# Layer 1's attention scores as pairs of 64-row tiles in fixed, adjacent PSUM banks

## The chip, the cores and the metric

The kernel runs on one core of one Trainium2 chip. The metric is device time in microseconds (us) of the whole program, the median of the runs shown. The engines go by short names: PE is TensorE's matrix multiply and PEld its weight load, DVE is VectorE, ACT is ScalarE, POOL is GpSimd; SP is the queue that issues all the DMAs here. PSUM is the memory that PE writes its results to and that DVE and ACT read them from.

## What is computed

Two transformer layers, each with an attention part and a feed-forward part, between modulated layer norms, over 2 sequences of 512 tokens with 512 channels. Layer 0's attention is a chunked linear attention (32 query heads of width 128 in 8 groups, chunks of 128 tokens) with a gate. Layer 1's is a plain softmax attention with 32 query heads of width 16, four of which share one of 8 key heads. Its feed-forward part mixes four streams with a 4x4 matrix that 50 Sinkhorn iterations make doubly stochastic. The change touches layer 1's attention:

```python
x = x + ga * attention0(h)                   # layer 0
x = x + gb * ffn0(layernorm(x) * (1 + cb) + sb)

xq = (x @ wq + bq).reshape(B, S, 32, 16)     # layer 1
xk = (x @ wk + bk).reshape(B, S, 8, 16)
xv = (x @ wv + bv).reshape(B, S, 8, 16)
q, k = _rope(xq, cos, sin), _rope(xk, cos, sin)
k, v = jnp.repeat(k, 4, axis=2), jnp.repeat(xv, 4, axis=2)
scores = jnp.einsum('bqhd,bkhd->bhqk', q, k) / jnp.sqrt(16.0)
probs = jax.nn.softmax(scores, axis=-1)
out = jnp.einsum('bhqk,bkhd->bqhd', probs, v)
...
H_res = sinkhorn_log(H_res_logits)           # 50 iterations, per token 4x4
```

## The kernel before

**Layer 0** runs as 64 units (L1305 and after): a unit is one group of four heads, one sequence and one chunk of 128 tokens. Every float product is made exact by three passes of rounded halves (`passes`, L227 to 234; the matmuls are all on L233). A unit asks for a gate tile (`gate`, PSUM name `gps`), for projections of queries, keys and values (`project`, `pps`), for scores (`sps`), a state (`cps`), a mixed output (`yps`), its transpose (`ztp`) and an output projection (`ops`). Each of these is one bank-sized PSUM tile of 128x512 floats, each name may have two at once, and all names share one pool: a scheduler, which plans the order of every engine's queue ahead of time from a model of the machine, gives a tile room when its first writer comes up and frees it after its last reader. `bank` (L155) is the helper through which `gps`, `pps`, `ops` and a few others are asked for. Weights come through staging tiles named `raw` (`raw_tile`, L199), of which there are `RAW` = 4: a DMA fills one, ACT rounds it to the high half (L210), POOL subtracts to get the low half (L211), and it is free again. `mod_load` (L266) takes up to four of them at once for the modulation rows.

**Layer 1's attention** runs as 128 pieces: two sequences, two halves of 256 queries, four pairs of key heads (`t`), and within each of these 16 steps eight pieces. Three pieces are put behind each of the last 11 units of layer 0, up to 33 (`FIRST`, `PER`, `HOLD`, L1343); the rest follow layer 0. A piece has two parts, and `weigh` runs ten pieces behind `maxima`.

`maxima` (L834) finds each query's largest score, which the softmax subtracts. The queries of two key heads lie in one tile of 96 partitions, 48 for each key head (high, high and low parts of 16 numbers), and each key head has a key tile of its own, zero in the other head's rows. So one matmul over 96 rows gives the scores of one key head, 128 queries by 512 keys, in a PSUM tile `s1` (three at once), and one DVE instruction (L847) reduces it:

```python
for qt in range(NQ):
    ps = psp.tile([P, L], FP, name="s1", bufs=S1)
    anchor["pe"] = nc.tensor.matmul(
        ps, lhsT=st["qs"][rp][0:KS, i, qt * P:(qt + 1) * P], rhs=st["ks"][s][0:KS], ...
```

A piece holds two such matmuls (two query tiles) and two reductions. After every fourth piece the maxima are split in two halves (L853, L854), transposed into `mt` (L857), copied by ACT to `mm` (L862) and written by one DMA (L863) into rows 96 to 99 of the query tile, where rows of ones in the key tile subtract them.

`weigh` (L865) makes the scores again, transposed, 128 keys by 256 queries at a time, over 100 rows (L877): per piece two PSUM tiles `s2` (three at once), each of two matmuls, and for each one ACT exponential (the `pt` rows on L68, the line of the helper that records ACT's instructions). `outputs` (L887, L897) multiplies four pieces' weights by the values, in four column tiles of 32 columns, into `op`; `finish` (L911) transposes that into `ot`, divides and adds it to the residual. `aside` (L1190) lets the Sinkhorn work of finished tokens run two steps per piece.

Of the kernel before, what the change touches and what calls it, by code (L numbers as in the profile page):

```python
# [21 lines left out]
RAW = 4  # L22
# [3 lines left out]
UPO = 600  # L26
SPLIT0, SPLIT1 = 16, 16
# [26 lines left out]
def tile_adaln(ctx: ExitStack, tc: tile.TileContext, a: dict, out: bass.AP):  # L54
# [62 lines left out]

    anchor = {}
# [35 lines left out]

    def bank(shape, name, bufs=2):  # L155
        return psp.tile(shape, FP, name=name, bufs=bufs)
# [576 lines left out]

    Q = L // 2
    NQ = Q // P
    KS, KM = 96, 100
# [4 lines left out]
    def layer1_keys(js=(0, 1)):  # L741
        for s in range(2):
            empty = temp([P, L], FR, "hi1")
            nc.scalar.copy(empty, raw_tile(a["c_keys1"][s]))
            for j in js:
                ksd[j, s] = temp([P, L], FR, f"ks{j}{s}")
                nc.sync.dma_start(out=ksd[j, s].bitcast(FP), in_=empty.bitcast(FP))
# [39 lines left out]
    def key_rows(i):  # L787
        j = key_tile(i)
        if j == 2 and (2, 0) not in ksd:
            layer1_keys((2,))  # L790
        return [ksd[j, s] for s in range(2)]

    def keys1(i):
        b, t = order[i]["b"], order[i]["t"]
        order[i]["ks"] = key_rows(i)
        holder[key_tile(i)] = i
        for s in range(2):
            nc.sync.dma_start(out=order[i]["ks"][s].bitcast(FP)[48 * s:48 * s + 48], in_=k_dram[b][2 * t + s])

    def queries1(i):  # L800

        b, half, t = (order[i][n] for n in ("b", "half", "t"))
        assert l1c["there", b]
        pair = []
        for rp in range(2):
            qs = temp([P, 2, Q], FR, "qs", QS)
            for s in range(2):
                h = 8 * t + 4 * s + 2 * rp
                nc.sync.dma_start(
                    out=qs.bitcast(FP)[48 * s:48 * s + 48],  # L810
                    in_=q_dram[b][h:h + 2, :, half * Q:half * Q + Q].rearrange("r k q -> k r q"),
                )
            pair.append(qs)
        return pair
# [18 lines left out]

    def maxima(st, k):  # L834

        assert holder[key_tile(st["i"])] == st["i"]
        rp, j = divmod(k, 4)
        s, i = divmod(j, 2)
        if j == 0:
            st["m"] = small.tile([P, NQ * 2, 2], FP, name="m")  # L840
        for qt in range(NQ):
            ps = psp.tile([P, L], FP, name="s1", bufs=S1)
            anchor["pe"] = nc.tensor.matmul(  # L843
                ps, lhsT=st["qs"][rp][0:KS, i, qt * P:(qt + 1) * P], rhs=st["ks"][s][0:KS],
                start=True, stop=True,
            ).ins
            anchor["dve"] = nc.vector.tensor_reduce(  # L847
                st["m"][:, 2 * qt + s, i:i + 1], ps, AX.X, ALU.max, negate=True
            ).ins
        if j == 3:  # L850
# [12 lines left out]
            anchor["sp"] = nc.sync.dma_start(out=st["qs"][rp].bitcast(FP)[96:100], in_=mm.bitcast(FP)).ins  # L863

    def weigh(st, k):  # L865

        assert holder[key_tile(st["i"])] == st["i"]
        rp, r = divmod(k, 4)
        kp, s = divmod(r, 2)
        if r == 0:  # L870
            quads.append({"st": st, "rp": rp, "pt": {}})
        qd = quads[-1]
        for i in range(2):
            ps = psp.tile([P, 2, Q], FP, name="s2", bufs=S2)
            for j in range(2):
                kt = 2 * kp + j
                nc.tensor.matmul(  # L877
                    ps[:, j, :], lhsT=st["ks"][s][0:KM, kt * P:(kt + 1) * P], rhs=st["qs"][rp][0:KM, i, :],
                    start=True, stop=True,
                )  # L880
# [6 lines left out]
    def outputs(j):  # L887
# [6 lines left out]
        with tc.high_priority(UPO):  # L894
            for kt in range(NC):
                for r in (3, 0, 1, 2):
                    mm = nc.tensor.matmul(  # L897
                        op[32 * r:32 * r + 32, :], lhsT=va[st["b"]][kt // 2][:, kt % 2, 2 * st["t"] + r // 2, :],
                        rhs=qd["pt"][r, kt // 2][:, kt % 2, :], start=kt == 0, stop=kt == NC - 1,
# [306 lines left out]
    at = [0]  # L1206
# [224 lines left out]
```

## Time and profile before

| | |
|---|---|
| three runs | 1408.99, 1407.75, 1398.83 us; median 1407.75 |
| the profiled execution | 1409.56 us, of which the trace's span is 1407.8 |
| mean granted TensorE clock | 0.944 of full |
| busy, share of the span | PE 89%, PEld 70%, DVE 83%, ACT 59%, POOL 56% |
| first and last maxima matmul (L843) | 898.4, 1261.4 us |
| first and last weighing matmul (L877) | 925.1, 1275.6 us |
| last matmul of layer 0 (`ops`) | 1033.8 us |

The same profile in 40 slices of 35.2 us, each digit the busy share in tenths:

```profile
PE   6979999999999999999988998899998899994117
DVE  7998668687677687787999977788699879888998
ACT  5456576476476466666665655567567467653226
PEclk9999999999999999999999999999999899986568
```

PE is at its top through layer 0 and through most of layer 1's attention. After 1276 us only the last tokens' Sinkhorn iterations and the last mixing are left, a stretch of 132 us in which DVE does most. A busy PE isn't the same as a PE that takes a new matmul as early as it can: a matmul's duration includes the time in which it runs through the array, and consecutive ones overlap. What a matmul costs the next one is the distance from start to start, which the timeline shows.

### The profile page before, as it was taken

To read this page: it belongs to the slowest core of one execution; us is meant where nothing else is said; L and a number is where in the kernel's file an instruction comes from. 1 tells how busy PE (TensorE), PEld (TensorE's weight loads), DVE (VectorE), ACT (ScalarE), POOL (GpSimd) and SP (SyncE) were. 2 spreads that over 40 slices of the span, in tenths; PEclk is the share of its full clock that TensorE was granted. 3 is DMA by queue.
4 is the path that set the end of the run, shared out by engine and by line. 5 is a ranking of instruction groups with operands and counts; after the bars stand their busy time and mean duration, and the time that the engine had idled before them with its cause. 6 is when DMAs were issued, how large, how long until landed. Compare 5 with 4: busy or idle time off the path is not lost. (4 is left out here: it accounts for less than half of the span.)

```text
span 1407.8 us, 23038 instructions
## 1 busy us (share of the span) xinstructions
PE 1247.3 (89%) x7128; PEld 990.5 (70%) x7128; DVE 1164.4 (83%) x3171; ACT 825.1 (59%) x2333; POOL 787.2 (56%) x1180
## 2 busy tenths in 40 slices
PE   6979999999999999999988998899998899994117
PEld 3767888788788778888876777677776667762116
DVE  7998668687677687787999977788699879888998
ACT  5456576476476466666665655567567467653226
POOL 4363274365264367577777757644243644657854
PEclk9999999999999999999999999999999899986568
DMA  7121241231131233224333327623212331100001
GB/s 241 36 70 43 87 124 39 68 106 53 53 118 56 94 117 111 81 79 128 120 106 90 98 70 233 179 66 97 65 42 94 101 92 48 59 2 1 1 15 46
DMA packets 95378, 117.14 MB, mean 83 GB/s; under 512 B 10828, under 2 KB 50508, under 8 KB 95256
## 3 DMA queue, kind: packets, MB, share of 16 engines
q1 hardware_dynamic: 95256, 115.67, 27.6%
q8 instruction: 57, 0.93, 0.3%
q14 instruction: 65, 0.53, 0.1%
HBM read 102.11 MB, written 10.64 MB: 80 GB/s over the span
## 5 line engine op out<-in xcount | busy, mean ns | idle before, releaser
L847 DVE TENSOR_REDUCE m<-s 128x1 f32<-128x512 f32 x256 | 166.6, 673 | 21.8 <-PE s L843 21.5
L68 ACT ACTIVATE pt<-s 128x512 f32<-128x512 f32 x256 | 137.4, 601 | 33.1 <-PE s L877 31.5
L448 POOL TENSOR_TENSOR q<-xcos,rot 128x512 f32<-128x512 f32 x64 | 92.8, 1450 | 56.5 <-DVE xcos L446 52.5
L68 ACT ACTIVATE sg<-sg 128x512 f32<-128x512 f32 x128 | 80.7, 632 | 64.5 <-DVE sg L479 62.5
L496 POOL TENSOR_SCALAR_AFFINE_SELECT dec<-gb 128x512 f32<-128x512 f32 x64 | 48.3, 755 | 121.2 <-DMA gb<-g_dram 65.4
L843 PE MATMUL s<-ks,qs 96*128 96x512 f32 x256 | 104.9, 442 | 11.5 <-DVE m L847 7.6
L877 PE MATMUL s<-qs,ks 100*128 100x256 f32 x512 | 104.4, 309 | 10.2 <-DMA qs<-mm 6.8
L233 PE MATMUL pps<-hh,wq_h 128*128 128x512 f32 x256 | 103.3, 403 | 7.1 <-ACT vT L767 3.4
L877 PEld LDWEIGHTS s<-qs,ks 100*128 100x128 f32 x512 | 82.7, 199 | 32.8 <-issue 7.9
L68 ACT ACTIVATE dec<-dec,room 128x128 f32<-128x128 f32 x256 | 83.0, 398 | 34.8 <-POOL dec L496 34.6
L233 PE MATMUL ops<-wo_h,zh 128*128 128x512 f32 x256 | 102.2, 399 | 1.2 <-ACT zh L571 1.0
L233 PE MATMUL gps<-wg_h,hh 128*128 128x512 f32 x256 | 101.3, 398 | 1.5 <-ACT wg_h L210 1.2
L233 PE MATMUL ops<-wo_h,zl 128*128 128x512 f32 x256 | 101.5, 396 | 0.7 <-DVE zl L572 0.7
L233 PE MATMUL pps<-hl,wq_h 128*128 128x512 f32 x256 | 101.8, 398 | 0.0
L233 PE MATMUL pps<-hh,wq_l 128*128 128x512 f32 x256 | 101.5, 397 | 0.0
L233 PE MATMUL gps<-wg_l,hh 128*128 128x512 f32 x256 | 101.1, 395 | 0.0
L233 PE MATMUL ops<-wo_l,zh 128*128 128x512 f32 x256 | 100.6, 393 | 0.0
L233 PE MATMUL gps<-wg_h,hl 128*128 128x512 f32 x256 | 100.6, 393 | 0.0
L516 POOL TENSOR_TENSOR gb<-gb,q 128x512 f32<-128x512 f32 x48 | 62.3, 1299 | 60.3 <-ACT gb L68 46.7
L549 PE MATMUL yps<-v,dec 128*128 128x128 f32 x512 | 93.4, 278 | 2.7 <-DVE xcos L446 1.4
L555 ACT ACTIVATE z<-yps 128x128 f32<-128x128 f32 x256 | 67.5, 278 | 41.1 <-PE yps L551 30.5
L559 DVE SCALAR_TENSOR_TENSOR z<-yps,ss,sg 128x128 f32<-128x128 f32 x256 | 72.0, 340 | 22.5 <-ACT ss L68 22.3
(321 smaller groups left out, 3984.4 us busy)
## 6 DMA issues: line engine op xcount, KB each, us to landing
gb<-g_dram SPq DMA_DIRECT2D x64, 256.0 KB
raw<-in_wq SPq DMA_DIRECT2D x56, 256.0 KB
raw<-in_wg SPq DMA_DIRECT2D x48, 256.0 KB
raw<-in_wo SPq DMA_DIRECT2D x48, 256.0 KB
raw<-in_wmod SPq DMA_DIRECT2D x40, 256.0 KB
qs<-q_dram SPq DMA_DIRECT2D x64, 96.0 KB
q_dram<-hi SPq DMA_DIRECT2D x16, 256.0 KB
raw<-in_wk SPq DMA_DIRECT2D x14, 256.0 KB
```

The costliest lines, as they stand in the source:

```text
L68: ins = nc.scalar.activation(o, i, func, **kw)
L233: nc.tensor.matmul(ps, lhsT=l, rhs=r, start=i == 0, stop=i == n - 1)
L448: nc.gpsimd.tensor_tensor(dst, sp(xc_), sp(rot), ALU.add)
L496: anchor["pool"] = nc.gpsimd.affine_select(out=dec, in_=gb, pattern=[[0, REP0], [1, P]], compare_op=ALU.is_ge, fill=-1e30, base=0, channel ...
L516: nc.gpsimd.tensor_tensor(gb, gb, q[:, c], ALU.mult)
L549: nc.tensor.matmul(yps[:, h, :], lhsT=u["pr"][:, h, :], rhs=u["v"][:, c, :], start=True, stop=not c)
L555: nc.scalar.activation(z[:, h, :], yps[:, h, :], AF.Square, accum_out=ss[:, h:h + 1])
L559: nc.vector.scalar_tensor_tensor(z[:, h, :], yps[:, h, :], ss[:, h:h + 1], sg[:, h * P:(h + 1) * P], ALU.mult, ALU.mult)
L843: anchor["pe"] = nc.tensor.matmul(ps, lhsT=st["qs"][rp][0:KS, i, qt * P:(qt + 1) * P], rhs=st["ks"][s][0:KS], start=True, stop=True,).ins
L847: anchor["dve"] = nc.vector.tensor_reduce(st["m"][:, 2 * qt + s, i:i + 1], ps, AX.X, ALU.max, negate=True).ins
L877: nc.tensor.matmul(ps[:, j, :], lhsT=st["ks"][s][0:KM, kt * P:(kt + 1) * P], rhs=st["qs"][rp][0:KM, i, :], start=True, stop=True,)
```

## The change

The two key heads of a step move to two halves of one tile: head 0 in partitions 0 to 47, head 1 in 64 to 111, with the rows of the maxima and of ones in 48, 49 and 112, 113. A matmul now works on 48 (or 50) rows that start at partition 0 or 64, and the two heads' matmuls follow each other directly, each into a bank of its own. The key tiles become half as many.

In `maxima` a piece is one pair of matmuls, one for each key head, of the same query tile, and one reduction over both banks gives both maxima. In `weigh` a piece is one pair, each 128 keys by 512 columns (two query heads at once) in place of four matmuls of 256 columns. The maxima go out by two DMAs, one for each half.

The reduction needs the two banks to lie side by side, so two pairs of banks, `pair0` and `pair1`, are set aside for the whole program. Until the first piece, the gate's tiles (`gps`) take turns in the two banks of `pair0`; until piece 48 (`ROOM2`), the projections' (`pps`) take turns in `pair1`. Pieces 0 to 47 use `pair0` alone, the later ones both in turn. The staging tiles `raw` go from four to three.

```diff
-RAW = 4
+RAW = 3
+ROOM2 = 48
...
+    pairs2 = [psp.tile([P, 2, L], FP, name=f"pair{k}", bufs=1) for k in range(2)]
+    turn2 = [0, 0]
     def bank(shape, name, bufs=2):
+        k = {"gps": 0, "pps": 1}.get(name)
+        if k is not None and (n_done[0] == 0 if k == 0 else n_done[0] < ROOM2):
+            turn2[k] += 1
+            return pairs2[k][:, turn2[k] % 2]
         return psp.tile(shape, FP, name=name, bufs=bufs)
...
-    KS, KM = 96, 100
+    KS, KM = 48, 50
...
-            nc.sync.dma_start(out=order[i]["ks"][s].bitcast(FP)[48 * s:48 * s + 48], in_=k_dram[b][2 * t + s])
+            nc.sync.dma_start(out=order[i]["ks"].bitcast(FP)[64 * s:64 * s + KS], in_=k_dram[b][2 * t + s])
...
+    def score_room(n):
+        return pairs2[n % 2 if n >= ROOM2 else 0]
     def maxima(st, k):
...
-        s, i = divmod(j, 2)
+        i, qt = divmod(j, 2)
...
-        for qt in range(NQ):
-            ps = psp.tile([P, L], FP, name="s1", bufs=S1)
+        pss = score_room(8 * st["i"] + k)
+        for s in range(2):
             anchor["pe"] = nc.tensor.matmul(
-                ps, lhsT=st["qs"][rp][0:KS, i, qt * P:(qt + 1) * P], rhs=st["ks"][s][0:KS],
-                start=True, stop=True,
+                pss[:, s], lhsT=st["qs"][rp][64 * s:64 * s + KS, i, qt * P:(qt + 1) * P],
+                rhs=st["ks"][64 * s:64 * s + KS], start=True, stop=True,
             ).ins
-            anchor["dve"] = nc.vector.tensor_reduce(
-                st["m"][:, 2 * qt + s, i:i + 1], ps, AX.X, ALU.max, negate=True
-            ).ins
+        anchor["dve"] = nc.vector.tensor_reduce(
+            st["m"][:, 2 * qt:2 * qt + 2, i], pss, AX.X, ALU.max, negate=True
+        ).ins
...
-            anchor["sp"] = nc.sync.dma_start(out=st["qs"][rp].bitcast(FP)[96:100], in_=mm.bitcast(FP)).ins
+            for s in range(2):
+                anchor["sp"] = nc.sync.dma_start(
+                    out=st["qs"][rp].bitcast(FP)[64 * s + KS:64 * s + KM], in_=mm.bitcast(FP)[4 * s:4 * s + 4]
+                ).ins
     def weigh(st, k):
...
-        for i in range(2):
-            ps = psp.tile([P, 2, Q], FP, name="s2", bufs=S2)
-            for j in range(2):
-                kt = 2 * kp + j
-                nc.tensor.matmul(
-                    ps[:, j, :], lhsT=st["ks"][s][0:KM, kt * P:(kt + 1) * P], rhs=st["qs"][rp][0:KM, i, :],
-                    start=True, stop=True,
-                )
+        pss = [psp.tile([P, 2, Q], FP, name="s2", bufs=S2) for s in range(2)]
+        for s in range(2):
+            nc.tensor.matmul(
+                pss[s], lhsT=st["ks"][64 * s:64 * s + KM, kt * P:(kt + 1) * P], rhs=st["qs"][rp][64 * s:64 * s + KM],
+                start=True, stop=True,
+            )
+        for s in range(2):
             p = wts.tile([P, 2, Q], FP, name="pt", bufs=PT)
-            anchor["act"] = qd["last"] = act(p, ps, AF.Exp, scale=0.25)
-            qd["pt"][2 * s + i, kp] = p
+            anchor["act"] = qd["last"] = act(p, pss[s], AF.Exp, scale=0.25)
+            qd["pt"][s, kt] = p
...
-    at = [0]
+    at = n_done
```

More of the change, by code (lines that the diff above doesn't have):

```diff
@@ L116, in rsqrt @@
         nc.vector.tensor_tensor(dst, dst, t, ALU.mult)
+    n_done = [0]
     anchor = {}
@@ L741, in layer1_keys @@
     def layer1_keys(js=(0, 1)):
[L742 to L747, printed above, removed]
+        empty = temp([P, L], FR, "hi1")
+        nc.scalar.copy(empty, raw_tile(a["c_keys1"][0]))
+        for j in js:
+            ksd[j] = temp([P, L], FR, f"ks{j}")
+            for s in range(2):
+                nc.sync.dma_start(
+                    out=ksd[j].bitcast(FP)[64 * s + KS:64 * s + KM], in_=empty.bitcast(FP)[96:98]
+                )
     steps = [(g, b) for g in range(KV0 - AHEAD) for b in range(B)]
@@ L788, in key_rows @@
         j = key_tile(i)
-        if j == 2 and (2, 0) not in ksd:
+        if j == 2 and 2 not in ksd:
             layer1_keys((2,))
-        return [ksd[j, s] for s in range(2)]
+        return ksd[j]
     def keys1(i):
@@ L809, in queries1 @@
                 nc.sync.dma_start(
-                    out=qs.bitcast(FP)[48 * s:48 * s + 48],
+                    out=qs.bitcast(FP)[64 * s:64 * s + KS],
                     in_=q_dram[b][h:h + 2, :, half * Q:half * Q + Q].rearrange("r k q -> k r q"),
@@ L862, in maxima @@
             nc.scalar.copy(mm, mt)
[L863 removed]
+            for s in range(2):
+                anchor["sp"] = nc.sync.dma_start(
+                    out=st["qs"][rp].bitcast(FP)[64 * s + KS:64 * s + KM], in_=mm.bitcast(FP)[4 * s:4 * s + 4]
+                ).ins
     def weigh(st, k):
         assert holder[key_tile(st["i"])] == st["i"]
[L868 to L870 removed]
+        rp, kt = divmod(k, 4)
+        if kt == 0:
             quads.append({"st": st, "rp": rp, "pt": {}})
         qd = quads[-1]
[L873 to L880 removed]
+        pss = [psp.tile([P, 2, Q], FP, name="s2", bufs=S2) for s in range(2)]
[3 more added lines that the diff above has]
+                start=True, stop=True,
+            )
+        for s in range(2):
             p = wts.tile([P, 2, Q], FP, name="pt", bufs=PT)
[L882 to L883 removed]
+            anchor["act"] = qd["last"] = act(p, pss[s], AF.Exp, scale=0.25)
+            qd["pt"][s, kt] = p
     quads = []
@@ L898, in outputs @@
                         op[32 * r:32 * r + 32, :], lhsT=va[st["b"]][kt // 2][:, kt % 2, 2 * st["t"] + r // 2, :],
-                        rhs=qd["pt"][r, kt // 2][:, kt % 2, :], start=kt == 0, stop=kt == NC - 1,
+                        rhs=qd["pt"][r // 2, kt][:, r % 2, :], start=kt == 0, stop=kt == NC - 1,
                     ).ins
```

## The prediction

> **What bounds the kernel now.** I read the busy shares by stage first, cut where the work changes: pure layer 0, the stretch in which layer 1's pieces run beside it (from 898 us), attention beside the second sequence's feed-forward (from 1033 us), attention alone (1116 to 1276 us), and the end.
>
> ```profile
> core 0: us, PE busy (x) PEld busy (x) DVE busy (x) ACT busy (x) POOL busy (x), PEclk, DMA share, GB/s
> 150.00:650.00 500.00, 497.92 (x2568) 409.79 (x2567) 374.75 (x757) 306.40 (x890) 272.90 (x225) 1.00 0.29 86
> 650.00:898.00 248.00, 226.92 (x1098) 185.16 (x1097) 214.00 (x391) 145.82 (x414) 177.61 (x142) 0.97 0.43 127
> 898.00:1033.00 135.00, 126.40 (x763) 99.73 (x762) 115.16 (x255) 85.75 (x245) 55.61 (x53) 0.96 0.27 74
> 1033.00:1116.00 83.00, 79.28 (x581) 58.11 (x580) 80.17 (x213) 53.66 (x136) 38.58 (x47) 0.98 0.24 74
> 1116.00:1276.00 160.00, 146.56 (x1225) 103.66 (x1227) 132.56 (x463) 105.48 (x250) 89.77 (x326) 0.91 0.19 57
> 1276.00:1408.00 132.00, 44.68 (x292) 40.87 (x284) 119.39 (x780) 45.69 (x162) 87.83 (x335) 0.65 0.05 17
> ```
>
> The columns are the stretch, its length, then busy us and instructions of each engine. Layer 0 to 650 us is PE alone. From 1033 to 1116 us DVE is at 97% (80.17 of 83). From 1116 us nobody is full: DVE has 132.56 of 160, and what it waits for is in the waits of that stretch (us in total, times, longest):
>
> ```profile
> DVE m L847 <- PE s L843: 18.7, 19, 3.1
> ...
> PE s L877 <- DMA qs<-mm: 6.8, 8, 2.1
> ```
>
> DVE waits 18.7 us for maxima matmuls that stand in PE's queue behind others, and PE waits 5.1 us for DVE's reductions. So this stage is held by PE's order, and DVE comes right behind. The groups to be changed (busy, mean ns of one, idle before):
>
> ```profile
> L847 DVE TENSOR_REDUCE m<-s 128x1 f32<-128x512 f32 x256 | 166.6, 673 | 21.8 <-PE s L843 21.5
> L843 PE MATMUL s<-ks,qs 96*128 96x512 f32 x256 | 104.9, 442 | 11.5 <-DVE m L847 7.6 <-DVE st L538 2.2 <-DMA raw<-in_ffwT 1.1
> L877 PE MATMUL s<-qs,ks 100*128 100x256 f32 x512 | 104.4, 309 | 10.2 <-DMA qs<-mm 6.8 <-ACT pt L68 1.1 <-DVE zl L572 0.8
> L897 PE MATMUL op<-pt,va 128*32 128x256 f32 x1024 | 68.9, 412 | 0.5 <-ACT pt L68 0.5
> L1109 DVE TENSOR_REDUCE sinkhorn<-sinkhorn 128x8 f32<-128x32 f32 x196 | 31.8, 167 | 1.0
> ```
>
> Durations mislead for PE, so its timeline (start, duration) around two changes of shape:
>
> ```profile
> 86.83 0.43 PE L424 MATMUL gtp<-room,e 32*128 32x32 f32 x4
> 87.19 0.50 PE L233 MATMUL pps<-hh,wq_h 128*128 128x512 f32 x1
> 87.53 0.40 PE L233 MATMUL pps<-hl,wq_h 128*128 128x512 f32 x1
> 87.76 0.39 PE L233 MATMUL pps<-hh,wq_l 128*128 128x512 f32 x1
> ...
> 1179.78 0.39 PE L843 MATMUL s<-ks,qs 96*128 96x512 f32 x1
> 1180.01 0.42 PE L877 MATMUL s<-qs,ks 100*128 100x256 f32 x2
> 1180.27 0.40 PE L843 MATMUL s<-ks,qs 96*128 96x512 f32 x1
> 1180.60 1.94 PE L897 MATMUL op<-pt,va 128*32 128x256 f32 x32
> ```
>
> A matmul of 512 columns takes 0.23 us from start to start, two of 256 columns 0.26 us (0.24 when more follow), whatever the durations say. The 32 column-tile matmuls of `op` take 1.94 us, 0.24 for each four: matmuls in different column tiles do overlap. Entering such a shape costs 0.33 instead of 0.23 (1180.27 to 1180.60). Behind the four transposes of 32 rows (86.83) the first two full matmuls stand 0.34 apart instead of 0.23. I put a stay in another tile shape at 0.10 for entering, 0.11 for the late second matmul behind it, and as much again as entering, 0.09, for leaving: 0.30 us.
>
> **PE.** Today the scores cost 256 x 0.23 + 512 x 0.12 = 120 us of PE's queue. If two 64-row tiles overlap as column tiles do, 256 pairs cost 0.24 each, 61 us. But scores stand among other shapes: the trace has 41, 31 and 66 unbroken runs of score matmuls in the three attention stages, and each run is to cost 0.30 us. Score tiles alone, the stages hold 66, 52 and 139 maxima matmuls and 86, 110 and 315 weighing ones. So:
> - 898 to 1033: before 66 x 0.23 + 86 x 0.12 = 25.5; after 54 pairs x 0.24 + 41 x 0.30 = 25.3. Nothing.
> - 1033 to 1116: 25.2 against 53 x 0.24 + 31 x 0.30 = 22.0, and DVE binds there.
> - 1116 to 1276: 69.8 against 148 x 0.24 + 66 x 0.30 = 55.3: 14.5 us less asked of PE.
>
> [...]
>
> **DVE.** A reduction of 32 numbers takes 167 ns and one of 512 takes 673, so 1.05 ns a number and 1.21 us for 1024. Two now have 2 x 166.6 / 256 = 1.30 us of busy time. That saves 0.09 us a piece: 2.3 us in 1033 to 1116 (26 pieces), 6.2 us in 1116 to 1276 (69). Bounds: 1.08 us (1024 x 1.05 ns and no start) to 1.35 (two whole instructions), so 0.22 saved to 0.05 lost a piece, 21 us to -5 us over 95 pieces. I take 0.09, from the two rows that are nearest.
>
> **Attention's sum.** 1033 to 1116 follows DVE: -2. In 1116 to 1276, -6 from DVE's own time, and of its 18.7 us of waits three quarters, -14, about what PE is spared. ACT is no bound (105 of 160; its exponentials keep number and size). Against it stands the second DMA of the maxima: two issues of the neighbouring query loads take 0.84 us, so about 0.42 later landing, and PE waits for that DMA eight times here: +3. Total -19. Bounds: 0 if DVE's waits only change their name; if DVE were full from 1033 on, 243 - (212.7 - 8.5) = -39.
>
> **PSUM.** From start of first matmul to end of last read I counted in the trace how many tiles are alive; it is never over eight, which I take as the number of rooms. Four go to the pairs. What must share the other four (all but `gps`, `pps` and, from 898 us, all but `pps` and `s1`) is over four during 3% of 150 to 650 us, 23% of 650 to 898, 19% of 898 to 1033 and 2% later. So where PE is full, four do; from 650 to 1033 us PE can run ahead less. There DVE has 86% and PE about 92%, and much of the crowding is tiles waiting for a late DVE, so I charge +2. Its end above is a stall for all of that time, 0.23 x 248 + 0.19 x 135 = 83 us; below, nothing. `pair0` alone for pieces 0 to 47 means matmul, reduction, matmul in sequence, some 0.4 + 1.2 us with nothing beside; those 48 pieces now take 176 us (to 1074), 3.7 us each, so other work covers it. Without cover it would be 0.4 us x 48 = 19 us of DVE.
>
> **RAW.** Waits of PE for weight halves are 1.2 us in all (the `gps` matmuls on the late high half), so one staging tile less costs little. The eight modulation jobs of four rows must split their matmuls, since the fourth row's load waits on SP for the first matmul; what is queued behind it on SP are other staging loads and the decay rows (POOL waits 65.4 us for those now, mostly off PE's path). One more tile-shape stay each: 8 x 0.30 = 2.4. I charge +2; a late start of the program could add 3. The fewer key-tile loads lie under other work: nothing.
>
> Sum: -19 + 2 + 2 = -15 on the profiled 1409.6, so 1394.6. The median is 1.8 below that execution: **1393**.
>
> **Rivals.**
> 1. *Even* (1404, within 1%). Pairs overlap, but DVE's waits turn into waits for `ot`, the maxima DMA or ACT; only DVE's own -8 stays and layer 0 gives 4 back. For it: DVE at 97% in one stage; the chain of waits goes through PE, ACT and the maxima DMA in turn. Against it: 18.7 us of DVE's idle time name the very matmul that gets shorter.
> 2. *Slower by rooms* (1430). Four rooms hold PE up from 650 to 1033 us. If two fifths of the 83 us stall, +33, and the full attention gain of -15 (with the DMA and raw terms) is outweighed: +18 to +22. It decides from about 15 us lost, 18% of the crowded time. For it: `pair1` is reserved for `pps`, which my count has at 0.2 rooms on average from 898 us. Against it: up to 650 us four suffice, and DVE paces much of the rest.
> 3. *Row tiles don't overlap* (1433). Then 512 score matmuls cost 118 us as before and the shape changes add 138 x 0.30 = 41, some three fifths of it on the path, 25. The change wouldn't do what it says. Against it: column tiles overlap in every `op` run. It shows as 0.23 us between the starts of a pair.
>
> **Numbers.** Chances: forecast 0.43, even 0.30, rooms 0.19, no overlap 0.08. About 1%, 14 us, is what a measurement of this kernel tells from no change (the three runs lie 10 us apart). My forecast stands right at that edge, and its cases run down to the -39 bound (1369), so most of them, and a few of rival 1's, are faster by over 1%: 0.42 faster, 0.32 same, 0.26 slower. The range goes from 1372, short of the -39 bound, to 1430, where both slower cases begin; 1376 to 1406 for the forecast alone.
>
> **What would show it.** Right: the two starts of a pair a few ns apart, and a run of pairs at about 0.24 us each; reductions of 1.21 us; DVE's wait for the maxima matmul well under 18.7 us; attention after the last `ops` matmul some 19 us shorter; that last matmul at 1033 to 1040 us. Wrong: a last `ops` matmul after 1050 us (rooms), reductions of 1.3 us or more, pairs 0.23 us apart, or as much DVE idle time under another name.

## The result, and the profile after

The changed kernel takes **1504.76 us** (median of four runs, 1498.18 to 1510.06) beside 1406.32 us (four runs) for the kernel before: ratio **1.0707, 95% interval 1.0647 to 1.0767**. It is 7% slower; 1393 was predicted.

The profiled execution has a span of 1502.6 us, 94.8 more than before. Busy times by stage (columns as before), cut at the same events: unit 52 at 861 us, the first piece at about 900, the last `ops` matmul at 1094 (before 1033.8), the last weighing matmul at 1366 (before 1275.6).

```profile
core 0: us, PE busy (x) PEld busy (x) DVE busy (x) ACT busy (x) POOL busy (x), PEclk, DMA share, GB/s
118.50:861.00 742.50, 718.17 (x3609) 583.81 (x3608) 570.01 (x1138) 445.07 (x1298) 418.37 (x344) 0.99 0.29 85
900.00:1094.00 194.00, 170.82 (x843) 117.31 (x843) 141.16 (x268) 101.11 (x282) 75.76 (x70) 0.89 0.28 83
1094.00:1366.00 272.00, 245.54 (x1576) 126.19 (x1578) 219.07 (x667) 163.18 (x387) 146.75 (x478) 0.82 0.19 56
```

From the last `ops` matmul to the last weighing matmul the kernel before took 242 us at a clock of 0.94; here it is 272 us at 0.82. Neither PE (245.54 of 272) nor DVE (219.07) is full. The clock has its own line in the page, in 40 equal slices; first the kernel before, then the changed one:

```profile
PEclk9999999999999999999999999999999899986568
```

```profile
PEclk9889999999999999999999999989878879977656
```

Apart from the last slices, where PE has little to do in either kernel, the losses of clock lie at the start and in the slices of attention. In the traces of these two kernels every record of the clock is full or half, and those at half (19 before, 34 after the change) last 3.41 us or 2 to 17 times that, but for one that the end of the trace cuts short in each. Between the last `ops` and the last weighing matmul the kernel before spends 31 us at half clock, the changed one 95; between unit 52 and the last `ops` it is 14 us before and 44 after.

The groups that answer to those of before:

```profile
L865 DVE TENSOR_REDUCE m<-pair 128x2 f32<-128x1024 f32 x128 | 154.3, 1209 | 23.9 <-PE pair L861 17.8 <-PE s L895 5.5
L895 PE MATMUL s<-qs,ks 50*128 50x512 f32 x256 | 103.8, 525 | 15.6 <-ACT pt L69 6.2 <-DMA qs<-mm 2.7 <-ACT os L928 2.3
L861 PE MATMUL pair<-ks,qs 48*128 48x512 f32 x256 | 79.9, 527 | 12.8 <-DVE m L865 7.0 <-DMA ks<-k_dram 3.4 <-DMA qs<-q_dram 2.0
L916 PE MATMUL op<-pt,va 128*32 128x256 f32 x1024 | 82.6, 469 | 2.9 <-ACT pt L69 1.9 <-ACT ht L194 0.8
```

The one reduction takes 1209 ns, as forecast. But `op`, which the change doesn't touch, has gone from 68.9 to 82.6 us for the same 1024 matmuls. The timeline of PE shows why (start, duration, matmuls, idle time before):

```profile
1222.05 0.50 PE L861 MATMUL pair<-ks,qs 48*128 48x512 f32 x2 [0.79 <-DVE m L865]
1222.39 0.40 PE L895 MATMUL s<-qs,ks 50*128 50x512 f32 x2
1223.25 0.50 PE L861 MATMUL pair<-ks,qs 48*128 48x512 f32 x2 [0.47 <-DVE m L865]
1223.68 0.44 PE L937 MATMUL ot<-room,os 128*128 128x128 f32 x2
...
1225.58 0.50 PE L861 MATMUL pair<-ks,qs 48*128 48x512 f32 x2
1226.42 0.79 PE L895 MATMUL s<-qs,ks 50*128 50x512 f32 x1 [0.34 <-ACT pt L69]
1226.78 0.86 PE L861 MATMUL pair<-ks,qs 48*128 48x512 f32 x2
1227.37 0.62 PE L895 MATMUL s<-qs,ks 50*128 50x512 f32 x1
1227.93 3.64 PE L916 MATMUL op<-pt,va 128*32 128x256 f32 x32
```

Before, the same 32 matmuls took:

```profile
1173.39 1.93 PE L897 MATMUL op<-pt,va 128*32 128x256 f32 x32
```

The run of 32 falls into a stretch at half clock (1226.05 to 1232.88 us) and takes 3.64 us instead of 1.93. Two pairs one behind the other start 0.34 us apart, 1222.05 to 1222.39, where 0.24 was forecast. Durations run past the next start here as before (there 0.39 us at a step of 0.23 for 512 columns, 0.28 at 0.12 for 256).

The single rows (x1) in these lines are no gaps in the record: all 256 maxima and all 256 weighing matmuls are there. They are pairs that the plan has pulled apart. Of the 512 score matmuls 316 start within 20 ns of another one: 83 times two maxima matmuls, 39 times two weighing matmuls, 36 times one of each. The other 196 start alone. Counted in order of time, the two matmuls of a maxima pair stand next to each other in PE's order 117 of 128 times, and 81 of these start within 20 ns; of the weighing pairs 53 do, and 24 start so.

The waits between the last `ops` and the last weighing matmul (total, times, longest), first in the kernel before:

```profile
ACT pt L68 <- PE s L877: 25.8, 30, 3.0
DVE m L847 <- PE s L843: 19.9, 20, 3.1
```

```profile
ACT pt L69 <- PE s L895: 30.0, 41, 3.1
...
DVE m L865 <- PE pair L861: 8.8, 9, 1.8
...
DVE m L865 <- PE s L895: 5.5, 4, 2.5
PE pair L861 <- DVE m L865: 5.3, 8, 2.2
```

DVE's reductions wait 8.8 us for maxima matmuls, and 5.5 us more that the profile puts down to a weighing matmul: 14.3 us, where it was 19.9. Over the whole kernel nothing is won, as the line of L865 above shows: 17.8 and 5.5 us, beside 21.5 before. What was saved behind the last `ops` came back ahead of it, where the pieces use `pair0` alone.

In layer 0 PE has a wait that it hardly had before (4.0 us, three times, for the same reader); over the whole kernel:

```profile
PE pair L243 <- DVE xcos L456: 29.5, 13, 6.0
```

The projections wait for the readers of the fixed `pair1`, whose halves go round in the order in which they were asked for.

By stage, the 94.8 us are: +8.7 up to unit 0's `ops` (118.5 us), +23.7 from there to unit 52, +27.7 from unit 52 to the last `ops`, +29.6 from there to the last weighing matmul, +5.0 at the end.

### The profile page after: what moved, and what is told of

The parts are those of the page before. It is cut to its first block, busy times and chain, and to the rows that moved or that the text cites. A ratio compares the mean times of both kernels' runs of the same rounds, so it can differ in the third digit from the quotient of the medians.

```text
span 1502.6 us, 22438 instructions
## 1 busy us (share of the span) xinstructions
PE 1303.0 (87%) x6872; PEld 959.9 (64%) x6872; DVE 1165.8 (78%) x3043; ACT 831.7 (55%) x2330; POOL 781.5 (52%) x1180
## 5 line engine op out<-in xcount | busy, mean ns | idle before, releaser
L865 DVE TENSOR_REDUCE m<-pair 128x2 f32<-128x1024 f32 x128 | 154.3, 1209 | 23.9 <-PE pair L861 17.8
L895 PE MATMUL s<-qs,ks 50*128 50x512 f32 x256 | 103.8, 525 | 15.6 <-ACT pt L69 6.2
L243 PE MATMUL pair<-hh,wq_h 128*128 128x512 f32 x256 | 104.3, 407 | 11.9 <-DVE xcos L456 11.5
L1180 PE MATMUL mix<-h,dg 128*128 128x128 f32 x192 | 35.1, 335 | 81.9 <-ACT dg L1179 81.8
L243 PE MATMUL pair<-hh,wq_l 128*128 128x512 f32 x256 | 101.6, 397 | 0.0
L243 PE MATMUL pair<-hl,wq_h 128*128 128x512 f32 x256 | 101.1, 395 | 0.0
L243 PE MATMUL pair<-wg_h,hh 128*128 128x512 f32 x220 | 88.2, 401 | 6.7 <-DVE sg L492 6.7
L519 DVE SCALAR_TENSOR_TENSOR dec<-sps,room,dec 128x128 f32<-128x128 f32 x256 | 73.1, 342 | 24.6 <-PE sps L243 12.4
L861 PE MATMUL pair<-ks,qs 48*128 48x512 f32 x256 | 79.9, 527 | 12.8 <-DVE m L865 7.0
L559 PEld LDWEIGHTS yps<-v,dec 128*128 128x128 f32 x512 | 80.9, 198 | 12.0 <-issue 3.7
```

The costliest lines, as they stand in the source:

```text
L243: nc.tensor.matmul(ps, lhsT=l, rhs=r, start=i == 0, stop=i == n - 1)
L519: anchor["dve"] = nc.vector.scalar_tensor_tensor(dec[:, h, :], sps[:, h, :], dtc[:, c, r0 + h:r0 + h + 1], dec[:, h, :], ALU.mult, ALU.mul ...
L559: nc.tensor.matmul(yps[:, h, :], lhsT=u["pr"][:, h, :], rhs=u["v"][:, c, :], start=True, stop=not c)
L861: anchor["pe"] = nc.tensor.matmul(pss[:, s], lhsT=st["qs"][rp][64 * s:64 * s + KS, i, qt * P:(qt + 1) * P], rhs=st["ks"][64 * s:64 * s + K ...
L865: anchor["dve"] = nc.vector.tensor_reduce(st["m"][:, 2 * qt:2 * qt + 2, i], pss, AX.X, ALU.max, negate=True).ins
L895: nc.tensor.matmul(pss[s], lhsT=st["ks"][64 * s:64 * s + KM, kt * P:(kt + 1) * P], rhs=st["qs"][rp][64 * s:64 * s + KM], start=True, stop= ...
```

## The experiments

Three theories were set against each other. **1**: the reserved rooms, and the fixed order that two named banks force. **2**: the 64-row tiles, which was then split into *2a*, the clock follows how much of PE's array is at work, and *2b*, it follows the time in which any matmul runs, or the shape changes cost the time. **3**: the missing staging tile. The first four runs take the change apart.

**before_raw3**, the staging tile alone:

```diff
-RAW = 4
+RAW = 3
```

> The kernel before with three staging tiles for raw weights instead of four, and nothing else. Theory 1 (the reserved rooms and the strict order that two fixed banks force cost the time) and theory 2 (the 64-row tiles cost it, by the clock that TensorE is granted when it is less busy and by the shape changes) both leave this at 1402 to 1412 us. Theory 3 (the missing staging tile costs a good part of it, at the start and wherever weights are converted): 1415 to 1435 us, with layer 0's first unit beginning at 116 us or later instead of 110.

Measured 1418.52 us, ratio 1.0085 [1.0062, 1.0108] to 1407.95 us. So 11 us, at the lower end of theory 3's range: a part, but a small one of 98. In the trace 7.5 us of it lie ahead of unit 0's `ops` matmul (117.3 us); from there to unit 52 it takes 718.9 us, as before (719.0).

**rooms_l0_48**, the reservation alone:

```diff
+    pairs2 = [psp.tile([P, 2, L], FP, name=f"pair{k}", bufs=1) for k in range(2)]
...
+        k = {"gps": 0, "pps": 1}.get(name)
+        if k is not None and (n_done[0] == 0 if k == 0 else n_done[0] < ROOM2):
+            turn2[k] += 1
+            return pairs2[k][:, turn2[k] % 2]
```

> The kernel before, with the change's reservation for layer 0 alone: gps in the fixed tile pair0 until the first piece, pps in the fixed tile pair1 until piece 48; the scores stay 96 rows deep with rooms of their own from the shared pool (which then has four), four staging tiles. Theory 1: 1435 to 1470 us, the last ops matmul at 1060 us or later (before 1034), PE waiting 15 us or more for readers of pair1. Theory 2: 1400 to 1420 us, the last ops matmul before 1045 us. Theory 3: as theory 2.

Measured 1448.01 us, 1.0294 [1.0270, 1.0318]: theory 1 holds for this part. The last `ops` matmul is at 1072.7 us, and of the 43 us of the profiled run 30 arise between unit 52 and it. The trace has two parts in these 30: PE stands idle for 33 us there (16 before), and 48 us of the stretch are at half clock (14 before), though the scores have 96 rows. Its PE waits over the whole kernel have the line of the changed kernel:

```profile
PE pair L242 <- DVE xcos L455: 20.3, 13, 4.2
```

Only 7.1 of these 20.3 us lie between unit 52 and the last `ops`. (The expectation counts four rooms for all others. That holds until the first piece; then `pair0` has had its last reader and is free, so there are six. In the trace five tiles of `s1`, `s2`, `mt`, `op`, `ot` and `ops` are alive at once beside the pieces, and seven behind the last `ops`, when `pair1` is free too.)

**tiles_only_s3**, the 64-row tiles alone, with rooms and reductions as before:

```diff
-    KS, KM = 96, 100
+    KS, KM = 48, 50
...
+        pss = [psp.tile([P, L], FP, name="s1", bufs=S1) for s in range(2)]
+        for s in range(2):
...
+                pss[s], lhsT=st["qs"][rp][64 * s:64 * s + KS, i, qt * P:(qt + 1) * P],
+                rhs=st["ks"][64 * s:64 * s + KS], start=True, stop=True,
```

> The kernel before with the 64-row tiles in both kinds of score matmuls and nothing else of the change: no fixed banks, four staging tiles, two separate reductions of 512 each. Theory 1: 1385 to 1415 us, the clock from the last ops matmul to the last weighing matmul at 0.90 or more. Theory 2: 1440 to 1470 us, that stretch 260 us or longer (before 242, changed 271) at a clock of 0.80 to 0.86 (before 0.93, changed 0.82), and the layer 0 units that run beside the pieces late too: last ops matmul at 1050 us or later. Theory 3: as theory 1.

Measured 1454.05 us, 1.0335 [1.0305, 1.0364]. Theory 2: the stretch after the last `ops` takes 274.8 us with 99 us at half clock. The last `ops` matmul, at 1045.4, is a little earlier than theory 2 had it.

**wide_rows**, the whole change without the 64-row tiles:

```diff
-                pss[:, s], lhsT=st["qs"][rp][64 * s:64 * s + KS, i, qt * P:(qt + 1) * P],
-                rhs=st["ks"][64 * s:64 * s + KS], start=True, stop=True,
+                pss[:, s], lhsT=st["qs"][rp][0:KS, i, qt * P:(qt + 1) * P],
+                rhs=st["ks"][s][0:KS], start=True, stop=True,
...
```

> The changed kernel with the 96-row and 100-row score matmuls of before, one after the other, each pair of maxima matmuls still into the two halves of a fixed pair and one reduction of 1024 for both; rooms, ROOM2 and three staging tiles as changed. Theory 1: 1475 to 1505 us, little better than the changed kernel. Theory 2: 1425 to 1455 us, the stretch from the last ops matmul to the last weighing matmul back at 235 to 248 us with a clock of 0.90 or more. Theory 3: 1480 or more.

Measured 1466.35 us, 1.0418 [1.0400, 1.0437], between the two. The stretch after the last `ops` is back at 246.1 us and a clock of 0.94, as theory 2 says; what is left, 58 us, is theory 1 and 3. Tiles and the rest of the change nearly add up: 46 + 58 = 104 for the two runs, and 98 for the changed kernel.

**Which part of the rooms.** rooms_l0_raw3 gives `pair1` free at the first piece, and has three staging tiles; wide_rows_both and both_from0 do the same to wide_rows and to the changed kernel, whose scores then take both pairs from piece 0:

```diff
-        if k is not None and (n_done[0] == 0 if k == 0 else n_done[0] < ROOM2):
+        if k is not None and n_done[0] == 0:
...
-        return pairs2[n % 2 if n >= ROOM2 else 0]
+        return pairs2[n % 2]
```

> The kernel before with three staging tiles and with gps and pps in the fixed pairs only until the first piece; scores as before. By the sums so far: 11 us for the staging tile. Theory 1 (the 30 us come from pps between the first piece and piece 48): 1418 to 1432 us, the stretch from unit 52 to the last ops matmul back at 205 to 212 us (234 with pps fixed until piece 48). Rival (the four free rooms): 1445 or more with that stretch at 225 or more. If the staging tile and the fixed order add to each other, unit 32 begins at 555 us or later (before 539, with three staging tiles alone 547, with fixed rooms and four tiles 536).

Measured 1438.56 us, 1.0230 [1.0192, 1.0267]: between the bounds, because two things happen. From unit 52 to the last `ops` it takes 210.3 us, so the 30 us go with `pps` in `pair1` beside the pieces. (The rival isn't tested here: with both pairs free from the first piece on, all eight rooms are shared.) But unit 52 begins at 853.3 us: 24 us late, where three staging tiles alone were 7 late and fixed rooms with four tiles 9. The two do more together than alone, and unit 32 at 553 us shows it, 2 us short of the bound set.

> The changed kernel with pair1 given up by pps at the first piece instead of at piece 48: scores take both pairs in turn from piece 0 on, pps comes from the shared pool. Theory 1 (the order that a fixed pps forces between the first piece and piece 48 costs 30 us): 1465 to 1482 us, PE waiting under 12 us for readers of pair1 (29.5 in the changed kernel), the last ops matmul at 1055 to 1072 us. Rival (it is the number of free rooms, four in either case, and not the fixed order): 1490 to 1510.

Measured 1509.31 us, 1.0726 [1.0685, 1.0768], in the rival's range. The theory's 1465 to 1482 fell: PE's wait for `pair1`'s readers is down to 17.9 us, yet from unit 52 to the last `ops` it takes 239 us, from there to the last weighing matmul 284.

> The changed kernel with the score matmuls 96 and 100 rows deep as before, and pair1 given up by pps at the first piece: scores take both pairs from piece 0, in the way of the changed kernel with one reduction of 1024, and everything else has four rooms. Theory: the stretch up to unit 52 as with three staging tiles and fixed rooms (853 us), the stretch from the last ops to the last weighing matmul 242 us as before. What is open is the stretch between: 205 to 213 us and 1435 to 1442 us if only pps in pair1 costs there; 220 us or more and 1445 to 1460 us if four free rooms cost as much.

Measured 1449.73 us, 1.0287 [1.0261, 1.0313], with 225.9 us from unit 52 to the last `ops`. So both cost. With `pps` in `pair1` and six rooms for the rest the stretch takes 235 us (rooms_l0_48), with `pps` free and four rooms left to all but the maxima 226, with neither 210. Lifting one alone leaves the other. The two don't add, though: wide_rows, which has both, takes 221.

**Is it the clock, and what does it follow?** To look for what a drop follows, windows of 3.41 us, on the grid on which the trace's records of the clock begin and end, were filled with the matmuls that start in them: columns of each matmul times its share of 128 rows times its share of 128 output columns, "full columns". The kernel before has a mean of 3973 to a window in attention, the changed one 2516. (8192, as in the next text, is what the fullest windows hold: 16 starts of 512 full columns, in three windows of the kernel before and two of the changed one. At 0.227 us from start to start a window mostly has room for 15 of these matmuls, 7680: 84 and 68 windows hold that.) The zero rows that the 64-row tiles got rid of were work to this count. tiles_full puts zero rows back into the small tiles: same instructions, same columns, more rows. The clearing of the query tile makes them zero:

```diff
-    KS, KM = 48, 50
+    KS, KM, KD = 62, 64, 48
...
+            nc.gpsimd.memset(qs.bitcast(FP), 0.0)
...
```

> The kernel with the 64-row tiles alone (1454 us), each tile now filled up with 14 rows of zeros: matmuls 62 and 64 rows deep instead of 48 and 50, as many of them and with as many columns; a clearing of each query tile on GpSimd comes in ahead of its loads. Theory 2a (the granted clock follows the share of the array's rows and columns at work: in the run with the tiles alone a window of 3.4 us with under 2300 of 8192 full columns was followed by a half clock 27 of 48 times, one above it 2 of 32): the stretch from the last ops to the last weighing matmul has 99 us at half clock in the run with the tiles alone; here 65 to 88, and 1435 to 1450 us in all. Theory 2b (the clock follows the time in which any matmul runs, however few its rows; or the shape changes cost the time): 92 us at half clock or more and 1450 to 1465 us.

Measured 1442.05 us, 1.0254 [1.0210, 1.0298], against 1.0335 [1.0305, 1.0364] for the tiles alone. The half clock fell to 65 us, as 2a has it.

tiles_cleared is its control, with the clearing but 48 and 50 rows:

> The control for the filled 64-row tiles: the same clearing of the query tiles and the same number of key transfers, but matmuls 48 and 50 rows deep as in the run with the tiles alone. Theory 2a: as the tiles alone, 1448 to 1460 us, 85 us or more at half clock from the last ops to the last weighing matmul. If the clearing or the order that was planned around it made the filled tiles faster: 1438 to 1446 us.

Measured 1467.27 us, 1.0408 [1.0373, 1.0444], above the range: the clearing, or the plan that came with it, costs some 10 us and gives nothing. Between control and filled tiles lie 22 us by the ratios. First the control's windows, then those of the filled tiles, from the last `ops` to the last weighing matmul:

```profile
1047.00:1330.00 283.00, 263.09 (x1584) 134.36 (x1583) 228.85 (x781) 164.48 (x390) 167.87 (x563) 0.82 0.18 54
```

```profile
1050.00:1308.00 258.00, 243.07 (x1581) 127.42 (x1581) 222.73 (x734) 162.28 (x391) 146.96 (x451) 0.87 0.19 59
```

As many matmuls (1584 and 1581), more rows, a clock of 0.87 instead of 0.82, and a stretch 25 us shorter. 2b can't say that. The order of PE's matmuls isn't the same in the two, as the scheduler plans each kernel anew, so the stretch is taken apart here. PE's steps from start to start, without the idle time that the trace shows, and with those at half clock counted half, are PE's work at full clock (from start to start, matmuls of 512 full columns take 0.426 us at half clock and 0.227 at full in before and in changed; short waits that hide behind a running matmul are in it): 215.5 us in the control, 213.9 with filled rows. The half clock adds 48.1 us to it in the one and 29.5 in the other: 19 of the 25 us. In the changed kernel itself the same pair of runs:

> The changed kernel with its tiles filled up with rows of zeros to 62 and 64 (and the clearing of the query tiles that this takes). Theory 2a: half clock from the last ops to the last weighing matmul 55 to 80 us instead of 96, and 1482 to 1497 us. If rows don't matter here: 1498 to 1515 us.

Measured 1463.48 us, 1.0416 [1.0388, 1.0445]; 61 us at half clock.

> The changed kernel with the clearing of the query tiles and as many key transfers as the one with filled rows, but matmuls 48 and 50 rows deep as changed: the control for after_full (1463 us). If the rows gave the 41 us: 1485 to 1510 us, 85 us or more at half clock from the last ops to the last weighing matmul, and at least 262 us for that stretch (271 changed, 253 with filled rows). If the clearing and its order gave them: 1460 to 1475 us. Up to 10 us less than the changed kernel's 1505 may come from another plan of the first 118 us alone.

Measured 1491.45 us, 1.0583 [1.0543, 1.0623]; 106 us at half clock. First the control's windows, then those of the filled tiles:

```profile
1090.00:1363.00 273.00, 250.14 (x1577) 127.98 (x1576) 217.02 (x630) 162.82 (x386) 157.34 (x498) 0.81 0.18 56
```

```profile
1073.00:1326.00 253.00, 230.76 (x1579) 120.74 (x1582) 212.46 (x606) 161.49 (x384) 151.79 (x467) 0.88 0.20 60
```

The stretch is 20 us shorter. PE's work in it is the same (202.8 and 202.5 us, counted as above), its idle time too (22.9 and 22.2); the half clock adds 46.8 us in the control and 27.8 with filled rows. By the ratios filled rows give 24 us against the control, and with them the changed kernel is where it is with the 96-row tiles (1466). In the profiled runs the two stages that hold score matmuls get 32 us shorter. Some 7 us lie elsewhere, though: the profiles of the changed kernel and its versions with three staging tiles have two different starts, with unit 0's `ops` at 117 to 119 us (before_raw3, changed, wide_rows, after_cleared) or at 108 to 111 (the five others, after_full too), and but for the rooms of layer 0 none of their edits touches what runs there. The scheduler plans every kernel anew. Its plan is worth up to 10 us here, and smaller differences between two of these kernels are not to be explained by their edits.

What of 2b is left, that it is PE's busy time that counts and not its rows, the windows of all 19 traces can answer. Taken are those of 3.41 us between the last `ops` and the last weighing matmul that are at full clock and in which PE is busy for over 95% of the time. With under 2300 full columns 16 of 40 had a half clock behind them, with 2300 to 3500 10 of 237, with more 0 of 459.

tiles_twice issues each maxima pair twice (`for s in (0, 1, 0, 1)`):

> The kernel with the 64-row tiles alone (1454 us), with each pair of maxima matmuls issued a second time into the same rooms: 128 pairs, some 38 us, more for PE. Theory 2a: the half clock from the last ops to the last weighing matmul falls from 99 us to 45 to 75, the op matmul's step from its mean of 91 ns to under 80, and the time stays within 15 us of the run with the tiles alone, 1440 to 1468. Theory 2b (shape changes and not the clock): the extra pairs are on top, 1475 to 1500 us, the clock no matter.

Measured 1475.94 us, 1.0496 [1.0458, 1.0534], 22 us above the tiles alone: out of 2a's range, and at 2b's lower end. Half clock is down to 75 us, as 2a has it. Working those 24 us off at half speed wins 12 of the 38; the rest is paid. It tells the theories apart poorly.

**Rooms for a pair.** tiles_only_s4 gives `s1` and `s2` four rooms each:

```diff
-S1, S2, MT, OT, OP = 3, 3, 2, 2, 2
+S1, S2, MT, OT, OP = 4, 4, 2, 2, 2
```

> The kernel with the 64-row tiles alone (1454 us), with four rooms each for s1 and s2 instead of three. Rival to theory 2a (a pair takes two of three rooms, so the next pair can't be started until both are read): 1425 to 1442 us. Theory 2a: 1446 to 1462 us, with 85 us or more at half clock.

Measured 1418.87 us, 1.0066 [1.0039, 1.0094]: better than the rival had it. The windows:

```profile
1049.00:1280.00 231.00, 222.48 (x1579) 118.40 (x1579) 208.93 (x648) 158.70 (x383) 119.36 (x340) 0.93 0.22 66
```

Forty-four us less than with three rooms, at a clock of 0.93, and 31 us at half clock instead of 99, where 2a said 85 or more. So in this stretch most of the half clock comes from small tiles and too few rooms together. (Ahead of it, from unit 52 to the last `ops`, four rooms don't help: 44 us at half clock, 34 with three.) In all, 35 us are won by the medians, as the stretch ahead and the end get longer. A pair takes two rooms at once, so with three the plan pulls pairs apart: two matmuls of a maxima pair stand next to each other in PE's order 40 of 128 times with three rooms and 93 times with four, those of a weighing pair 46 and 99 times. Its control, the kernel before with the same four rooms:

> The kernel before with four rooms each for s1 and s2 instead of three: the control for the 64-row tiles with four rooms (1419 us against 1454 with three). If three rooms are short only because a pair takes two at a time: 1400 to 1412 us, no change. If a fourth room helps whatever the tiles: 1370 to 1398 us, and then the tiles still cost 20 us or more.

Measured 1410.34 us, 1.0042 [1.0025, 1.0059]. The kernel before gains nothing by the fourth room in all: attention is 10 us shorter, the stretch ahead of it 9 longer and the end 8 longer. It has 17 us at half clock in attention. So three rooms are short mainly because of the pairs: 34 of the 44 us of attention are theirs. Even with four, the tiles bring nothing: 231 us of attention beside 232 without them.

> The 64-row tiles alone, filled up with rows of zeros and with four rooms each for s1 and s2. If the two causes add: 1394 to 1410 us, half clock from the last ops to the last weighing matmul under 20 us (31 with four rooms, 65 with filled rows, 99 with neither). If the missing rooms are the one cause and the half clock follows from PE's waits for them: 1412 to 1425 us, as with four rooms alone.

Measured 1421.75 us, 1.0128 [1.0099, 1.0157]: no better than four rooms alone, in the range of the second reading (the missing rooms as the one cause). Attention itself, at 225.7 us with 17 us at half clock, is the shortest of all runs, but the stretch ahead of it (221, before 205) and the end (142, before 132) take that back.

> The changed kernel with four rooms for s2 instead of three; maxima keep their fixed pairs. If the weighing pairs' three rooms cost the changed kernel's attention: the stretch from the last ops to the last weighing matmul 240 to 258 us instead of 271 and 1472 to 1492 us. If the four rooms that are left to all names are the limit, and not the three of s2: 1495 to 1512 us.

Measured 1484.99 us, 1.0564 [1.0532, 1.0596]. In the range of the first, for another reason: attention takes 267.8 us, only 4 less and not the 240 to 258 expected; 8 us are the other plan of the start. In the changed kernel the fourth room for `s2` helps little. The likely reason, not tested, is that `s2`, `mt`, `op` and `ot` share the four rooms that the fixed pairs leave.

**A version that is a little faster than both.** If full columns hold the clock up, the kernel before should gain by deeper matmuls. before_full fills its rows with zeros, 124 and 128 deep:

> The kernel before with its score matmuls filled up with zero rows, 124 and 128 deep instead of 96 and 100 (the maxima move to rows 124 to 127, the rows of ones with them), and a clearing of each query tile on GpSimd ahead of its loads. Theory 2a (the granted clock follows the share of the array at work): half clock from the last ops to the last weighing matmul falls from 31 us to 10 to 24, and 1392 to 1404 us, faster than before. Theory 2b (rows don't matter): 31 us at half clock, 1403 to 1412 us.

Measured 1405.11 us, **0.9976 [0.9961, 0.9990]**, 1 us above 2a's range and inside 2b's. The 3 us are clear of the noise of one kernel, but within what another plan is worth; the clock is the better witness. The half clock in attention fell from 31 to 7 us and the stretch from 242 to 232.6:

```profile
1039.00:1272.00 233.00, 216.29 (x1792) 156.09 (x1791) 211.54 (x668) 157.92 (x384) 138.99 (x397) 0.99 0.21 65
```

PE's order in that stretch is nearly the one of the kernel before. Its work at full clock is 212.8 us (210.9 before); the half clock adds 3.1 us to it instead of 13.8. About half of that is lost again between unit 52 and the last `ops`, which takes 210 us instead of 205.

The stages of the profiled runs side by side (us). The last four columns take the fourth stage, to the last weighing matmul, apart: the time at half clock, PE's work at full clock, what the half clock adds to it, and PE's idle time.

| kernel | to unit 0's `ops` | to unit 52 | to last `ops` | to last weighing | half clock | work | added | idle |
|---|---|---|---|---|---|---|---|---|
| before | 110 | 719 | 205 | 242 | 31 | 210.9 | 13.8 | 17.2 |
| before_raw3 | 117 | 719 | 206 | 242 | 24 | 211.9 | 11.7 | 18.0 |
| rooms_l0_48 | 112 | 726 | 235 | 245 | 27 | 211.6 | 12.8 | 20.3 |
| rooms_l0_raw3 | 110 | 743 | 210 | 242 | 27 | 211.9 | 12.0 | 18.1 |
| tiles_only_s3 | 110 | 718 | 217 | 275 | 99 | 208.4 | 48.0 | 18.4 |
| tiles_full | 110 | 719 | 221 | 258 | 65 | 213.9 | 29.5 | 14.9 |
| tiles_cleared | 111 | 718 | 218 | 284 | 102 | 215.5 | 48.1 | 19.9 |
| tiles_only_s4 | 110 | 717 | 222 | 231 | 31 | 207.8 | 14.9 | 8.5 |
| wide_rows | 119 | 743 | 221 | 246 | 27 | 217.4 | 13.4 | 15.3 |
| changed | 119 | 743 | 233 | 272 | 95 | 202.3 | 42.7 | 26.5 |
| after_full | 111 | 745 | 217 | 253 | 61 | 202.5 | 27.8 | 22.2 |
| after_cleared | 118 | 744 | 229 | 272 | 106 | 202.8 | 46.8 | 22.9 |

## Why the prediction was wrong

Two steps failed: the one from PE's spared work to time won, which leaves out the clock, and the +2 for PSUM. Each alone turns the forecast gain of 15 us into a loss: the tiles by themselves cost 46 us (tiles_only_s3), the reservation in layer 0 by itself 41 (rooms_l0_48).

**PE, the score pairs: mis-sized.** Row tiles do overlap: most of the maxima pairs that stand together start 3 to 4 ns apart. But where "256 pairs cost 0.24 each" two such pairs in a row stand 0.33 to 0.34 us apart; that is 1.4 times two in a row at 0.23, not 2 times. The 0.30 us for a stay was nearly right, and rather high: `ot` or `mt` to a pair takes 0.20 us (0.03 to a wide matmul), a pair to `op` 0.42 (0.33), `op` to a pair 0.31 as before. With 0.33 and 0.20 us the last stage's sum is 148 x 0.33 + 66 x 0.20 = 62 us instead of 69.8, so 8 us saved at best where 14.5 was taken. And the pairs don't stay pairs: the sum counts 256 of them, while 196 of the 512 matmuls start alone. From the last `ops` to the last weighing matmul PE's work at full clock fell by 9 us in all (210.9 to 202.3), where the prediction's two stages had 17.7; a part of the 9 is work done earlier, as 23% of the score matmuls ran ahead of the last `ops` and 20% before. That a pair of row tiles costs what column tiles cost in `op` was an estimate; the trace has 0.33 to 0.34 us in place of 0.24.

**The missing term: the clock.** This is the first step that failed. "-14, about what PE is spared" treats time spared on PE as time won. The columns above showed 0.91 for the last stage, and I read past it: work taken from PE there, zero rows included, cost speed. The half clock rose from 31 to 95 us. In the 29.6 us by which attention got longer PE's work is 9 us less, the half clock adds 29 us more (42.7, 13.8 before), and PE's idle time is 9 us longer. Filling the rows took 44 us of half clock and 20 us of the stretch off the changed kernel, against its control, at the same PE work: shown by runs with and without filled rows, in two kernels. It isn't the rows alone: the same small tiles with rooms for two pairs have 31 us at half clock (tiles_only_s4), where the wide ones have 17 (before_s4). Few rows and too few rooms make the drop together: 99 us (tiles_only_s3). What exactly sets the clock isn't shown.

**DVE: its own time right, its waits not.** 1.21 us forecast, 1209 ns measured. Its reductions' waits fell from 19.9 us to 14.3 behind the last `ops`, where "three quarters" were to go, and over the whole kernel they didn't fall. ACT now waits 30.0 us for the weighing matmuls (25.8 before). The second maxima DMA, charged at 3 us, isn't to be seen: PE waits 2.7 us for `mm` in all, 6.8 before.

**PSUM: right mechanism in rival 2, wrong size and wrong place.** This is the second step that failed. "So I charge +2" was too little by an order: the reservation alone costs 41 us by its ratio (rooms_l0_48). I counted the tiles alive in the old order as the demand. But the fixed pair also takes the order away: its halves go round in the order of asking, and the stretch beside the pieces takes 235 us with `pps` in it and 210 with the pair given up. That it is the order, and not that the eight rooms are split in six and two, is argued from the wait for `pair1`'s readers, which is 7.1 us there; the rest shows as other idle time of PE and as half clock. And for attention I wrote "2% later", which is the demand of single tiles; pairs take two rooms at a time. In the tiles alone three rooms for them cost 44 us of attention (275 against 231), where a fourth room gives the kernel before 10. Rival 2 had the loss right in kind, at 33 us, but for full gain elsewhere.

**`pair0` alone for pieces 0 to 47**: taken at nothing. With both pairs from piece 0 the changed kernel is no faster (both_from0), so no loss is shown; it wasn't tried by itself.

**RAW: mis-sized.** "I charge +2", with 3 more at the start as the far end; it is 11 us alone, 7.5 of it at the start. But five other versions with three staging tiles start at 108 to 111 us like the kernel before, so the 7.5 us may be the plan's and not the tile's. Together with the fixed rooms unit 52 is 24 us late, where 7 and 9 would make 16. Why the two do more together isn't settled: PE is busy all through that stretch and no single wait of it grows to that size.

**Rival 1** (even) fell, and **rival 3** too: row tiles do overlap, in part.

By the ratios, of 1407 us, and taken in this order, the 99 us come out as: 12 for the staging tile (before_raw3), 20 for fixed rooms in layer 0 on top of it (rooms_l0_raw3), 26 for the fixed pairs with one reduction and `pps` in `pair1` beside the pieces (wide_rows), 41 for the 64-row tiles, of which filled rows give 24 back against the control (7 of them at the start, which is the plan's).

## What to carry to other kernels

Here work taken off PE (210.9 to 202.3 us) was paid back by the clock: the time at half clock rose from 31 to 95 us, in a stage whose last part had a clock of 0.91 before, with PE busy for 146.56 of 160 us. So where a profile shows the like, look at how much of the array each stage keeps busy before calling a shorter matmul a saving, zero rows included. Small tiles with three rooms had 99 us at half clock (tiles_only_s3); small tiles with four (tiles_only_s4) and wide ones with three (before) had 31. A bank that is given a fixed name can cost more than its room, for it also fixes the order of those who ask for it: 41 us here for two pairs (rooms_l0_48). A step that takes two rooms at once wants four of them, or the plan pulls the two halves apart: 40 of 128 maxima pairs stand together with three, 93 with four. Look in the timeline whether pairs that were written together also start together; in the changed kernel 81 of 128 maxima pairs and 24 of 128 weighing pairs do. With a scheduler that plans anew, allow some 10 us for the plan, and test each part of a change on its own.

## What the runs showed of the hardware

- More rows of zeros in the same number of matmuls came with a higher granted clock between the last `ops` and the last weighing matmul: 0.87 beside 0.82 in the tiles alone (tiles_full, tiles_cleared), 0.88 beside 0.81 in the changed kernel (after_full, after_cleared), 0.99 beside 0.94 in the kernel before (before_full, before).
- In the changed kernel's attention a window of 3.41 us with fewer than 2300 full columns had a half clock behind it 25 of 44 times, one with more 4 of 36; in tiles_full_s4, 5 of 8 and 0 of 59.
- Among windows at full clock in which PE was busy for over 95% of the time, a half clock followed 16 of 40 with under 2300 full columns and 0 of 459 with over 3500, in the 19 traces.
- In the changed kernel two row tiles of 48 rows and 512 columns mostly start 3 to 4 ns apart where they stand next to each other in PE's order, and the next pair follows 0.33 to 0.34 us later.
